# Softmax normalisation on the probabilities, and modulation in four column groups, in a one-core AdaLN transformer block

## The chip, the cores and the metric

The kernel runs on one core of a Trainium2 chip. The metric is the time on the device in microseconds (us), the median of several runs. The engines are TensorE (PE; its weight loads are listed as PEld), VectorE (DVE), ScalarE (ACT), GpSimd (POOL) and SyncE (SP, which issues most DMA transfers). Each engine works through its own queue in order, and semaphores order the queues among each other.

## What is computed

The reference is one adaptive-layernorm block over x of shape 4 x 1024 x 512, all in float32. Cut to what matters here:

```python
mod = (silu(c) @ wmod).reshape(4, 6, 1, 512)          # c is 4 x 512
sa, ca, ga, sb, cb, gb = mod[:, 0], ..., mod[:, 5]
ga, gb = the same with absolute value at least 0.25
h = layernorm(x) * (1 + ca) + sa
q = h @ q_w.T + q_b        # 16 heads of 32
k, v = h @ k_w.T + k_b, h @ v_w.T + v_b   # one head of 32, shared by all 16
attn = softmax(causal(q k / sqrt(32)))
x = x + ga * ((attn v) @ o_w.T + o_b)
h = layernorm(x) * (1 + cb) + sb
x = x + gb * ffn(h)        # 512 -> 2 x 2048 -> 512, with Hadamard transforms and silu
```

The Hadamard transforms of the feed-forward are applied to its weights once, at the start of the kernel ("preparation").

## The kernel before

The rows of x are worked in 8 blocks of 512 (two per sequence), and each block in 4 query tiles of 128 rows. Attention takes its query tiles in units (class `Unit`): of 8 heads in block 0 and in the second block of each sequence, of 16 heads in the first blocks of the other sequences, 52 units in all. `kmax` is the number of keys that a tile sees, 128 to 1024. The unit's scores, 128 queries by `kmax` keys for each head, lie in one of two halves of the tile `p`.

The life of a unit goes through these streams:

- `scores` (L397): four heads at a time, PE multiplies in four row groups of 32 rows of the array into four PSUM banks. A new unit's scores wait until the unit before has been attended.
- `minima` (L418): DVE masks, negates and copies the scores from PSUM to `p`, and keeps the row minimum in `nm`.
- `exps` (L438): ScalarE exponentiates in place, head by head, and accumulates each row's sum into `den`.
- `turns` (L455): DVE transposes `p` in 32 x 32 squares, two heads at a time.
- `attend` (L482): PE multiplies by v in 16 tiles of 32 x 32; ScalarE copies the result to `oT` (L492).
- `finish`, once per query tile: PE folds four partial sums with the matrix `fold` (L520, four column groups). In parallel DVE takes the reciprocal of `den` (L510), POOL broadcasts it to 32 columns a head (`wrd`, L511), PE transposes that (L527) and ScalarE copies it out of PSUM (`rd`, L529). DVE multiplies both into `aT` (L531), and PE applies the output projection (L260, from `ow` and `aT`). `add` multiplies by the gate and adds to x on POOL.

Helper `full_mm` (L260) holds the accumulating matmuls of several streams: the kv and q projections, the output projection, the modulation, and gate and up of the feed-forward (`ps<-h2T,wgu`). The feed-forward runs over 16 halves of 256 rows, each in 16 steps: gate and up on PE, tanh on ScalarE (L824), two products on DVE (L826, L829), down on PE (L852). At most two gate steps may have a PSUM bank open.

In preparation the modulation matrix `wmod` comes in six parts of 512 x 512, one after the other with the weights, into three buffers in the second half of `p`. Stream `mods` computes four of the parts transposed (features on partitions: 16 matmuls with a moving operand of 4 columns, into `modT`) and two as rows (4 matmuls of 512 columns, the gates `ga` and `gb`). `butterflies` (L716) and `transforms` (L739 to L752) prepare the feed-forward's weights in two buffers `tmp`, and write them to DRAM.

The order of all this is not written out by hand. Every stream is a generator of operations `Op(engine, cost, emit, reads, writes)`, and the planner `Flow` picks while the kernel is built: among the operations that could start within 0.3 us of the earliest, on that operation's engine, the one with the lowest rank. Ranks are given to the streams at the end (`multiply` 0, `finish` 3, `minima` and `scores` 4, `turns` 7, `exps` 8, gate and up 12). Costs are estimates such as `act_cost(n)` = 0.285 + 0.00083 n us. Thus one changed operation moves others on all queues.

Of the kernel before, what the change touches and what calls it, by code (L numbers as in the profile page):

```python
# [16 lines left out]
B, S, D = 4, 1024, 512  # L17
H, HD = 16, 32
FF = 2048
P = 128  # L20
# [140 lines left out]
def adaln_block(ctx, tc, x_d, small_d, const_d, wmod_d, qwT_d, kwT_d, vwT_d, vb_d, owT_d, ob_d,  # L161
# [10 lines left out]
    def sb(name, *shape):  # L172
        return outer.tile([P, *shape], F32, name=name)
# [15 lines left out]
    modT = sb("modT", 4, NDC, B)  # L189
    sc2, bi2 = sb("sc2", NDC, B), sb("bi2", NDC, B)  # L190
    cg, wgh, qbs = sb("cg", NFC), sb("wgh", NFC), sb("qbs", NDC)
    scT = sb("scT", NDC, B)
    kT = sb("kT", S)
    vT = sb("vT", TB)
    vrep = sb("vrep", S // 32, HD)
# [10 lines left out]
    nm = sb("nm", NNM, 2, 4)  # L206
    den = sb("den", 4, H)
    oT = sb("oT", 4, H, 32)
    rden, wrd, rd = sb("rden", H), sb("wrd", D), sb("rd", D)
    aT = sb("aT", 2, NDC, P)  # L210
    ga, y, y2 = sb("ga", D), sb("y", 2, D), sb("y2", D)

# [39 lines left out]
    def bk(b):  # L252
        return ("bank", b)
# [122 lines left out]
            for h0 in range(0, H, heads):  # L376
                units.append(Unit(len(units), i, ql, h0, heads))

    to_min, to_exp, to_turn, to_attend = deque(), deque(), deque(), deque()
    n_group = [0]  # L380

    def scores():
# [45 lines left out]
    def exps():  # L428
        while True:
            yield until(to_exp, "minima")  # L430
            if not to_exp:
                break
            u, c, slot = to_exp.popleft()
            ds = (u.i * NT + u.ql) % 4
            for j in range(4):
                h = c * 4 + j - u.h0
                e = u.head(h)
                yield Op("ACT", act_cost(u.kmax) + 0.19, lambda: nc.scalar.activation(  # L438
                    e, e, AF.Exp, bias=nm[:, slot, u.t, j:j + 1], scale=-1.0,
                    accum_out=den[:, ds, c * 4 + j:c * 4 + j + 1]),  # L440
                    [("nm", slot, j)], [u.key(h), ("den", ds)])
                if j % 2:
                    to_turn.append((u, h - 1))
        over["exps"] = True

    def turns():


        while True:
            yield until(to_turn, "exps")  # L450
# [51 lines left out]
    def finish():  # L502

        while True:
            yield until(to_finish, "attend")
            if not to_finish:
                break
            i, ql = to_finish.popleft()
            ds, a = (i * NT + ql) % 4, ql % 2
            yield Op("DVE", 0.2, lambda: nc.vector.reciprocal(rden, den[:, ds, :]), [("den", ds)], ["rden"])  # L510
            yield Op("POOL", 0.62, lambda: nc.gpsimd.tensor_copy(  # L511
                wrd.rearrange("p (h d) -> p h d", d=HD), rden.unsqueeze(2).to_broadcast([P, H, HD])),
                ["rden"], ["wrd"])
            yield banks.have(2)
            bo, br = banks.take(2)

            def folds():
                for c in range(NDC):
                    for j, r in enumerate(rows):
                        nc.tensor.matmul(ps[r, bo, c * P:(c + 1) * P], fold, oT[:, :, 4 * c + j, :],  # L520
                                         start=True, stop=True)
            yield Op("PE", 0.95, folds, ["oT"], [bk(bo)], mode="cols")
            st.folded += 1

            def turn():
                for c in range(NDC):
                    nc.tensor.transpose(ps[:, br, c * P:(c + 1) * P], wrd[:, c * P:(c + 1) * P], ident)  # L527
# [108 lines left out]
    def mods():  # L636
        for _ in range(6):
            yield lambda: bool(to_mod)
            part, s = to_mod.popleft()
            wm = raws[s]  # L640
            yield banks.have(1)
            o, = banks.take(1)
            if part in (2, 5):
                g = part // 5
                pg = ps[0:4, o, :]
                yield Op("PE", mm(512, 4), lambda: full_mm(pg, [(scT[:, k, :], wm[:, k, :]) for k in range(NDC)]),
                         [("raw", s)], [bk(o)], mode="full")
                busy[s] = False
                yield lambda: any(tmp_free)
                ts = tmp_free.index(True)  # L650
                tmp_free[ts] = False
# [12 lines left out]
                yield Op("DVE", 3.5, emit, [bk(o)], [("tmp", ts)])  # L664
                yield load(0.01, gates_d[g], gate, [("gates", g)], [("tmp", ts)])
                tmp_free[ts] = True
            else:
                slot = {0: 0, 1: 1, 3: 2, 4: 3}[part]
                pm = ps[:, o, 0:NDC * B].rearrange("p (a b) -> p a b", b=B)

                def products():
                    for dc in range(NDC):
                        full_mm(pm[:, dc, :], [(wm[:, k, dc * P:(dc + 1) * P], scT[:, k, :]) for k in range(NDC)])
                yield Op("PE", 3.5, products, [("raw", s)], [bk(o)], mode="full")
                busy[s] = False
                yield Op("DVE", 0.2, lambda: nc.vector.tensor_scalar_add(modT[:, slot], pm, 1.0 if slot in (1, 3) else 0.0),
                         [bk(o)], [f"mod{part}"])
            banks.give(o)
# [181 lines left out]
    def outputs():  # L860
# [81 lines left out]
```

## Time and profile before

| | |
|---|---|
| median of 3 runs | 2203.12 us (2201.21 to 2204.9) |
| profiled execution | 2202.49 us |
| its span, first to last instruction | 2200.7 us |
| mean granted TensorE clock | 0.997 |
| ACT exponentials (L438) | 512, 391.1 us busy |
| PE transposes of `wrd` (L527) | 128, 273 ns median |
| DMA | 257.09 MB, mean 117 GB/s |

A line of the profile's groups reads: line, engine, operation, output<-inputs, shapes and number; then busy us in all and mean ns of one; then the engine's idle time just before them, and what ended most of it. In the timeline the first number is the start in us, the second the us it covers. A float32 matmul stands in the profile as two records, so four matmuls are eight records; a transpose is one. Busy times of PE overlap, because matmuls are pipelined; the distance from one start to the next is what PE spends. PEclk is the share of its full clock that TensorE was granted.

### The profile page before, as it was taken

The numbers are of one execution on the slowest core, as the hardware profiler recorded it, in microseconds if no ns is written. First come the engines' busy times: TensorE is split into PE (matmuls) and PEld (weight loads), VectorE is DVE, ScalarE is ACT, GpSimd is POOL, SyncE is SP. The second block draws the span as 40 slices with busy tenths as digits, with TensorE's granted clock in tenths as the row PEclk, the third lists the DMA queues.
The fourth block names the chain that finished last, engine by engine and source line by source line (L and its number), as shares of the span: only waits on it lengthen the run. The fifth ranks groups of instructions, "written<-read, shape, count | busy, mean of one in ns | idle before, by whom it ended". The sixth has DMA issues, their size and how long they took to land.

```text
span 2200.7 us, 41314 instructions
## 1 busy us (share of the span) xinstructions
PE 2172.7 (99%) x17264; PEld 1374.5 (62%) x17264; DVE 1156.3 (53%) x2691; ACT 745.7 (34%) x1739; POOL 196.7 (9%) x197
## 2 busy tenths in 40 slices
PE   7999999999999999999999999999999999999998
PEld 4545666566556666556766656656766666777776
DVE  2476757645746686265246666364236767122111
ACT  2464434335534343253134333442123343111000
POOL 1032001000110010011001001011000101000000
PEclk9999999999999999999999999999999999999999
DMA  7542423223313342232523223223523332355453
GB/s 241 205 146 86 155 92 111 97 92 101 97 58 97 109 132 87 68 109 89 172 87 103 95 88 121 82 92 115 178 95 102 111 98 92 124 163 159 157 158 109
DMA packets 115602, 257.09 MB, mean 117 GB/s; under 512 B 11724, under 2 KB 28236, under 8 KB 115416
## 3 DMA queue, kind: packets, MB, share of 16 engines
q1 hardware_dynamic: 112392, 251.76, 35.8%
q8 instruction: 136, 2.23, 0.4%
q10 hardware_dynamic: 3024, 2.69, 0.4%
q14 instruction: 50, 0.41, 0.1%
HBM read 233.42 MB, written 20.99 MB: 116 GB/s over the span
## 4 chain that ended last, share of the span: by engine, by line
PE 98%; DVE 1%; issue 0%; DMA 0%; ACT 0%; SPq 0%; POOLq 0%; POOL 0%; DVEq 0%; ACTq 0%
PE ps L260 54%; PE ps L852 21%; PE ps L482 8%; PE ps L397 7%; PE ps L520 1%; PE ps L289 1%; PE ps L745 1%; PE ps L746 1%; PE ps L527 1%; PE ps L739 1%; PE ps L742 1%; DMA p<-in_wmod 0%; DVE tmp L716 0%; DVE p L418 0%; DVE p L455 0%
## 5 line engine op out<-in xcount | busy, mean ns | idle before, releaser
L260 PE MATMUL ps<-h2T,wgu 128*128 128x256 f32 x4096 | 949.2, 382 | 0.0
L260 PEld LDWEIGHTS ps<-h2T,wgu 128*128 128x128 f32 x4096 | 765.2, 190 | 236.0 <-issue 136.5
L852 PE MATMUL ps<-wd,g 128*128 128x512 f32 x1024 | 488.2, 601 | 0.7 <-DVE p L455 0.7
L438 ACT ACTIVATE p<-p,nm 128x512 f32<-128x512 f32 (+7 forms) x512 | 391.1, 766 | 175.2 <-DVE nm L418 175.2
L824 ACT ACTIVATE th<-ps,wgh 128x256 f32<-128x256 f32 x256 | 121.4, 474 | 804.6 <-PE ps L260 789.9
L826 DVE SCALAR_TENSOR_TENSOR th<-th,ps 128x256 f32<-128x256 f32 x256 | 106.6, 416 | 518.6 <-ACT th L824 518.6
L455 DVE STREAM_TRANSPOSE p<-p 128x256 f32<-128x256 f32 (+7 forms) x256 | 342.8, 1362 | 22.8 <-ACT p L438 21.7
L418 DVE CUSTOM_DVE_ANT_0 p<-ps,maskw 128x512 f32<-128x512 f32 (+3 forms) x512 | 273.6, 585 | 117.3 <-PE ps L397 116.1
L852 PEld LDWEIGHTS ps<-wd,g 128*128 128x128 f32 x1024 | 186.4, 190 | 185.5 <-issue 166.5
L482 PE MATMUL ps<-p,vrep 32*32 32x256 f32 (+1 forms) x8256 | 193.6, 409 | 5.9 <-issue 5.4
L397 PE MATMUL ps<-kT,qT 32*128 32x512 f32 (+3 forms) x1536 | 180.0, 533 | 2.3 <-DVE nm L418 1.0
L482 PEld LDWEIGHTS ps<-p,vrep 32*32 32x32 f32 x8256 | 119.8, 103 | 75.5 <-issue 32.2
L418 DVE CUSTOM_DVE_ANT_0 p<-ps,maskw,nm 128x128 f32<-128x128 f32 (+3 forms) x256 | 126.9, 546 | 67.6 <-PE ps L397 66.9
L492 ACT COPY oT<-ps 128x256 f32<-128x256 f32 (+1 forms) x208 | 74.7, 432 | 184.2 <-PE ps L482 183.5
L829 DVE SCALAR_TENSOR_TENSOR g<-th,cg,ps 128x256 f32<-128x256 f32 x256 | 123.1, 481 | 9.0
L397 PEld LDWEIGHTS ps<-kT,qT 32*128 32x128 f32 x1536 | 61.2, 183 | 103.9 <-issue 76.0
L260 PE MATMUL ps<-hT,qw 128*128 128x512 f32 x256 | 119.3, 610 | 0.0
L260 PE MATMUL ps<-ow,aT 128*128 128x512 f32 x256 | 115.8, 595 | 0.0
L511 POOL COPY wrd<-rden 128x512 f32<-128x512 f32 x32 | 19.6, 612 | 880.7 <-DVE rden L510 772.2
L438 ACT ACTIVATION_READ_ACCUMULATOR p<-p,nm 128x1 f32 x512 | 96.5, 188 | 0.0
L877 POOL TENSOR_TENSOR xs<-xs,y 128x512 f32<-128x512 f32 x32 | 40.6, 1269 | 507.6 <-DVE y L872 507.6
L260 PEld LDWEIGHTS ps<-hT,qw 128*128 128x128 f32 x256 | 49.6, 196 | 54.4 <-issue 53.7
(82 smaller groups left out, 1017.0 us busy)
## 6 DMA issues: line engine op xcount, KB each, us to landing
wgu<-wgu_d SPq DMA_DIRECT2D x256, 512.0 KB, 3.3
wd<-wd_d SPq DMA_DIRECT2D x256, 256.0 KB, 2.7
xs<-in_x SPq DMA_DIRECT2D x32, 256.0 KB, 4.7
out<-xs SPq DMA_DIRECT2D x32, 256.0 KB, 2.5
p<-in_wmod SPq DMA_DIRECT2D x6, 1024.0 KB, 8.3
p<-in_wgT SPq DMA_DIRECT2D x4, 1024.0 KB, 6.8
p<-in_wupT SPq DMA_DIRECT2D x4, 1024.0 KB, 5.0
wgu_d<-wo SPq DMA_DIRECT2D x4, 1024.0 KB, 4.2
```

Of the source, the lines that this page charges most:

```text
L260: nc.tensor.matmul(out, l, r, start=(k == 0), stop=(k == len(pairs) - 1))
L397: nc.tensor.matmul(ps[:, bb[j], 0:n], qT[r, c, u.ql * P:(u.ql + 1) * P], kT[r, kb * 512:kb * 512 + n], start=True, stop=True)
L418: yield Op("DVE", 0.245 + 0.00103 * n, lambda: nc.vector.tensor_tensor_reduce(o, ps[:, bb[j], 0:n], m, -1.0, nm[:, slot, 0, j:j + 1] if kb ...
L438: yield Op("ACT", act_cost(u.kmax) + 0.19, lambda: nc.scalar.activation(e, e, AF.Exp, bias=nm[:, slot, u.t, j:j + 1], scale=-1.0, accum_ou ...
L455: yield Op("DVE", 0.135 + 0.00105 * 2 * u.kmax, lambda: nc.vector.transpose(e, e), [], [u.key(h), u.key(h + 1)])
L482: nc.tensor.matmul(ps[rows[c], bb[g], 0:w], vrep[rows[g], 4 * kt + c, :], pv[rows[g], :, k:k + 32], start=(kt == 0), stop=(kt == nkt - 1))
L492: yield Op("ACT", act_cost(w), lambda: nc.scalar.copy(oT[:, g, u.h0:u.h0 + u.heads, :], ps[:, bb[g], 0:w].rearrange("p (h q) -> p h q", q= ...
L824: yield Op("ACT", act_cost(HB), lambda: nc.scalar.activation(th, pg, AF.Tanh, scale=wgh[:, f:f + 1]), [bk(o)], [("th", ts)])
L826: yield Op("DVE", 0.46, lambda: nc.vector.scalar_tensor_tensor(th, th, 1.0, pg, ALU.add, ALU.mult), [bk(o)], [("th", ts)])
L829: yield Op("DVE", 0.46, lambda: nc.vector.scalar_tensor_tensor(g, th, cg[:, f:f + 1], pu, ALU.mult, ALU.mult), [bk(o), ("th", ts)], [("g", ...
L852: nc.tensor.matmul(ps[:, acc[j], :], ff["g"][:, k % NG, j * P:(j + 1) * P], ff["wd"][:, k % NWD, :], start=(f == 0), stop=(f == NFC - 1))
L877: yield Op("POOL", 1.3, lambda: nc.gpsimd.tensor_add(x, x, y2), ["y2"], [xk])
```

## The change

The softmax is normalised earlier. After the four exponentials of a group of heads DVE takes the reciprocals of their four sums, and a new stream `scales` multiplies the exponentials in place on ScalarE, one activation with a per-partition scale for each head, ahead of the transpose. `finish` then has nothing to multiply: a ScalarE copy brings the folded result to `aT`. The reciprocals of 16, the POOL broadcast, the four PE transposes, their ScalarE copy and the DVE product go.

The modulation is computed the other way round. For all six parts four matmuls stand side by side in four column groups, each with a 128-row chunk of the silu (padded with zeros to 32 columns) as the stationary operand and 512 columns of `wmod` as the moving one. ScalarE copies the four partial results to a `tmp` buffer, and a matmul with `fold` adds them up: one of 512 columns for the gates, four of 4 columns for the parts that are needed transposed. Each part now holds one of the two `tmp` buffers from the copy to its end.

```diff
-    scT = sb("scT", NDC, B)
+    scT = sb("scT", NDC, HD)
...
-    rden, wrd, rd = sb("rden", H), sb("wrd", D), sb("rd", D)
+    rden = sb("rden", 4, H)
...
-    nc.scalar.activation(scT.rearrange("p a b -> p (a b)"), small[:, C_CT:C_CT + 16], AF.Silu)
+    nc.gpsimd.memset(scT, 0.0)
+    nc.scalar.activation(scT[:, :, 0:B], small[:, C_CT:C_CT + 16].rearrange("p (a b) -> p a b", b=B), AF.Silu)
...
+            yield Op("DVE", 0.2, lambda: nc.vector.reciprocal(rden[:, ds, cols], den[:, ds, cols]),
+                     [dk], [("rden", ds, c)])
+            to_scale.append((u, c, ds))
+        over["exps"] = True
+
+    def scales():
+
+        while True:
+            yield until(to_scale, "exps")
+            if not to_scale:
+                break
+            u, c, ds = to_scale.popleft()
+            for j in range(4):
+                h = c * 4 + j - u.h0
+                e = u.head(h)
+                yield Op("ACT", act_cost(u.kmax), lambda: nc.scalar.activation(
+                    e, e, AF.Copy, scale=rden[:, ds, c * 4 + j:c * 4 + j + 1]),
+                    [("rden", ds, c)], [u.key(h)])
                 if j % 2:
                     to_turn.append((u, h - 1))
-        over["exps"] = True
+        over["scales"] = True
...
-            yield Op("DVE", 0.2, lambda: nc.vector.reciprocal(rden, den[:, ds, :]), [("den", ds)], ["rden"])
-            yield Op("POOL", 0.62, lambda: nc.gpsimd.tensor_copy(
-                wrd.rearrange("p (h d) -> p h d", d=HD), rden.unsqueeze(2).to_broadcast([P, H, HD])),
-                ["rden"], ["wrd"])
-            yield banks.have(2)
-            bo, br = banks.take(2)
+            yield banks.have(1)
+            bo, = banks.take(1)
...
-            def turn():
-                for c in range(NDC):
-                    nc.tensor.transpose(ps[:, br, c * P:(c + 1) * P], wrd[:, c * P:(c + 1) * P], ident)
-            yield Op("PE", 0.48, turn, ["wrd"], [bk(br)], mode="full")
-            yield Op("ACT", 0.6, lambda: nc.scalar.copy(rd, ps[:, br, :]), [bk(br)], ["rd"])
-            banks.give(br)
-            yield Op("DVE", 0.7, lambda: nc.vector.tensor_mul(
-                aT[:, a], ps[:, bo, :].rearrange("p (c q) -> p c q", c=NDC),
-                rd.rearrange("p (c q) -> p c q", c=NDC)), [bk(bo), "rd"], [("aT", a)])
+            yield Op("ACT", act_cost(512), lambda: nc.scalar.copy(
+                aT[:, a], ps[:, bo, :].rearrange("p (c q) -> p c q", c=NDC)), [bk(bo)], [("aT", a)])
...
+            def products():
+                for k, r in enumerate(rows):
+                    nc.tensor.matmul(ps[r, o, :], scT[:, k, :], wm[:, k, :], start=True, stop=True)
+            yield Op("PE", mm(512), products, [("raw", s)], [bk(o)], mode="cols")
+            busy[s] = False
+            yield lambda: any(tmp_free)
+            ts = tmp_free.index(True)
+            tmp_free[ts] = False
+            m = tmp[:, ts, 0, :]
+            yield Op("ACT", act_cost(512), lambda: nc.scalar.copy(m, ps[:, o, :]), [bk(o)], [("tmp", ts)])
...
-                yield Op("PE", mm(512, 4), lambda: full_mm(pg, [(scT[:, k, :], wm[:, k, :]) for k in range(NDC)]),
-                         [("raw", s)], [bk(o)], mode="full")
+                yield Op("PE", mm(512), lambda: nc.tensor.matmul(pg, fold[:, 0:B], m, start=True, stop=True),
+                         [("tmp", ts)], [bk(o)], mode="full")
...
-                def products():
+                def turned():
                     for dc in range(NDC):
-                        full_mm(pm[:, dc, :], [(wm[:, k, dc * P:(dc + 1) * P], scT[:, k, :]) for k in range(NDC)])
-                yield Op("PE", 3.5, products, [("raw", s)], [bk(o)], mode="full")
-                busy[s] = False
+                        nc.tensor.matmul(pm[:, dc, :], m[:, dc * P:(dc + 1) * P], fold[:, 0:B], start=True, stop=True)
+                yield Op("PE", 0.9, turned, [("tmp", ts)], [bk(o)], mode="full")
...
-        (7, turns), (8, exps), (5, butterflies), (4.5, transforms), (10, load_wgu), (10, load_wd),
+        (7, turns), (8, exps), (7.5, scales), (5, butterflies), (4.5, transforms), (10, load_wgu), (10, load_wd),
```

More of the change, by code (lines that the diff above doesn't have):

```diff
@@ L377, in adaln_block @@
                 units.append(Unit(len(units), i, ql, h0, heads))
-    to_min, to_exp, to_turn, to_attend = deque(), deque(), deque(), deque()
+    to_min, to_exp, to_scale, to_turn, to_attend = deque(), deque(), deque(), deque(), deque()
     n_group = [0]
@@ L434, in exps @@
             ds = (u.i * NT + u.ql) % 4
+            dk = ("den", ds, c)
+            cols = slice(c * 4, c * 4 + 4)
             for j in range(4):
@@ L440, in exps @@
                     accum_out=den[:, ds, c * 4 + j:c * 4 + j + 1]),
-                    [("nm", slot, j)], [u.key(h), ("den", ds)])
+                    [("nm", slot, j)], [u.key(h), dk])
+            yield Op("DVE", 0.2, lambda: nc.vector.reciprocal(rden[:, ds, cols], den[:, ds, cols]),
[14 more added lines that the diff above has]
+                    [("rden", ds, c)], [u.key(h)])
                 if j % 2:
                     to_turn.append((u, h - 1))
-        over["exps"] = True
+        over["scales"] = True
     def turns():
         while True:
-            yield until(to_turn, "exps")
+            yield until(to_turn, "scales")
             if not to_turn:
@@ L508, in finish @@
             i, ql = to_finish.popleft()
-            ds, a = (i * NT + ql) % 4, ql % 2
-            yield Op("DVE", 0.2, lambda: nc.vector.reciprocal(rden, den[:, ds, :]), [("den", ds)], ["rden"])
-            yield Op("POOL", 0.62, lambda: nc.gpsimd.tensor_copy(
-                wrd.rearrange("p (h d) -> p h d", d=HD), rden.unsqueeze(2).to_broadcast([P, H, HD])),
-                ["rden"], ["wrd"])
-            yield banks.have(2)
-            bo, br = banks.take(2)
+            a = ql % 2
+            yield banks.have(1)
+            bo, = banks.take(1)
             def folds():
@@ L645, in mods @@
                 pg = ps[0:4, o, :]
-                yield Op("PE", mm(512, 4), lambda: full_mm(pg, [(scT[:, k, :], wm[:, k, :]) for k in range(NDC)]),
-                         [("raw", s)], [bk(o)], mode="full")
-                busy[s] = False
-                yield lambda: any(tmp_free)
-                ts = tmp_free.index(True)
-                tmp_free[ts] = False
+                yield Op("PE", mm(512), lambda: nc.tensor.matmul(pg, fold[:, 0:B], m, start=True, stop=True),
+                         [("tmp", ts)], [bk(o)], mode="full")
                 sgn, mag, gate = (tmp[0:4, ts, j, :] for j in range(3))
@@ L665, in mods @@
                 yield load(0.01, gates_d[g], gate, [("gates", g)], [("tmp", ts)])
-                tmp_free[ts] = True
             else:
@@ L669, in mods @@
                 pm = ps[:, o, 0:NDC * B].rearrange("p (a b) -> p a b", b=B)
-                def products():
+                def turned():
                     for dc in range(NDC):
-                        full_mm(pm[:, dc, :], [(wm[:, k, dc * P:(dc + 1) * P], scT[:, k, :]) for k in range(NDC)])
-                yield Op("PE", 3.5, products, [("raw", s)], [bk(o)], mode="full")
-                busy[s] = False
+                        nc.tensor.matmul(pm[:, dc, :], m[:, dc * P:(dc + 1) * P], fold[:, 0:B], start=True, stop=True)
+                yield Op("PE", 0.9, turned, [("tmp", ts)], [bk(o)], mode="full")
                 yield Op("DVE", 0.2, lambda: nc.vector.tensor_scalar_add(modT[:, slot], pm, 1.0 if slot in (1, 3) else 0.0),
                          [bk(o)], [f"mod{part}"])
+            tmp_free[ts] = True
             banks.give(o)
```

## The prediction

> **What bounds the kernel now.** I read the page's first part, then the chain that ended last, then the waits of PE.
>
> ```profile
> PE 2172.7 (99%) x17264; PEld 1374.5 (62%) x17264; DVE 1156.3 (53%) x2691; ACT 745.7 (34%) x1739; POOL 196.7 (9%) x197
> PE 98%; DVE 1%; issue 0%; DMA 0%; ACT 0%; SPq 0%; POOLq 0%; POOL 0%; DVEq 0%; ACTq 0%
> ```
>
> ```profile
> PE ps L260 <- DMA p<-in_wmod: 11.5, 1, 11.5
> PE ps L482 <- issue: 5.4, 10, 1.6
> ```
>
> PE is busy 2172.7 of 2200.7 us, the chain is 98% PE, and apart from the first load (11.5 us) and the last outputs PE waits a few us in all. So a us of PE work removed is a us won, as long as PE gets no new waits. ScalarE (ACT) has 1455 us free, VectorE (DVE) 1044.
>
> A busy PE may still run slowly. A table of stretches shows where:
>
> ```profile
> core 0: us, PE busy (x) PEld busy (x) DVE busy (x) ACT busy (x) POOL busy (x), PEclk, DMA share, GB/s
> 11.45:32.00 20.55, 19.83 (x83) 17.19 (x84) 2.55 (x6) 3.80 (x8) 4.00 (x2) 1.00 0.70 245
> 54.00:74.00 20.00, 20.00 (x83) 12.88 (x82) 2.74 (x12) 1.70 (x2) 0.00 (x0) 0.74 0.53 181
> 100.00:150.00 50.00, 49.91 (x379) 22.80 (x378) 33.28 (x84) 33.49 (x87) 10.29 (x7) 1.00 0.59 192
> 150.00:200.00 50.00, 48.46 (x398) 26.09 (x408) 46.89 (x75) 26.38 (x61) 20.10 (x12) 1.00 0.28 85
> ```
>
> From 54 to 74 us PE is busy throughout, yet its granted clock is 0.74. The timeline there:
>
> ```profile
> 55.10 3.63 PE L260 MATMUL ps<-scT,p 128*128 128x4 f32 x32
> 58.59 5.38 PE L260 MATMUL ps<-hT,qw 128*128 128x512 f32 x8
> 63.81 4.62 PE L260 MATMUL ps<-scT,p 128*128 128x4 f32 x32
> 68.28 6.04 PE L260 MATMUL ps<-hT,qw 128*128 128x512 f32 x8
> ```
>
> The two projections (qw) take 5.22 and 5.98 us from start to next start; from 41.37 to 44.80, with the clock at 1.00, eight such records take 3.43. The slow clock follows the modulation's 128x4 matmuls. Below I cost PE work from start to next start, since busy times overlap.
>
> **What leaves PE.**
>
> The transposed reciprocals. In the timeline:
>
> ```profile
> 550.25 1.08 PE L520 MATMUL ps<-oT,fold 128*32 128x128 f32 x32
> 551.26 0.66 PE L527 MATMUL ps<-ident,wrd 128*128 128x128 f32 x4
> 551.76 3.62 PE L260 MATMUL ps<-h2T,wgu 128*128 128x256 f32 x16
> ```
>
> The four L527 transposes hold PE 0.50 us, 32 times: **16.0 us**. The POOL broadcast (L511, 19.6 us) and a reciprocal of 16 go too. The ScalarE copy to rd (586 ns x32) is replaced by a ScalarE copy to aT of the same size, so the fold's way to the output projection loses the DVE product (688 ns) and gains nothing.
>
> Modulation. Its six parts hold PE 6.82, 6.83, 4.70, 3.49, 4.47 and 3.52 us = 29.8. In the changed kernel each has four matmuls in four column groups. No 512-column one of these is in the trace; the nearest is the row-tiled L397, 1.07 us for eight records (702.49 to 703.56). L520 above speaks for overlap in column groups: its 32 records take 1.01 us, where L527's pace of 0.125 each would make 4.0. Bounds: 0.86 (one full matmul of 512, two records) and 3.43 (no overlap); I take 1.07, and twice that while the clock is at half, as it is for the first three parts. Then four parts have four 128x4 matmuls, eight records at 109 ns (3.49 / 32) = 0.87 us, two have one fold of 512 columns = 0.86. Sum: 2 x (2.14 + 1.75) + (2.14 + 1.72) + 2 x (1.07 + 0.87) + (1.07 + 0.86) = 17.4. Saved **12.4 us**.
>
> Clock. The two slow projections lose 5.22 + 5.98 - 2 x 3.43 = 4.3 us. The Trainium skill (TensorE: Matmul & The Clock Gate, Part 1) says that the gate follows how busy PE was in a window of about 3.4 us. By that rule a PE that is 100% busy would not slow down and I would book nothing; the row has 20.00 of 20.00 busy at 0.74. I read it as 128x4 matmuls counting as little work; the changed kernel has a quarter as many. Ends 0 and 4.3; I take **2**.
>
> The changed kernel's own PE order has 535 changes of tile shape for 540. One costs about 0.1 us (eight gate records 1.82 us beside a change, 5.18 / 3 = 1.73 without): **0.5**.
>
> Together PE is relieved of 30.9 us.
>
> **What is added, and where it lies.**
>
> The scales: 512 ScalarE copies with a per-partition scale, 64 each of 128 to 1024 columns in steps of 128. Nearest row:
>
> ```profile
> L824 ACT ACTIVATE th<-ps,wgh 128x256 f32<-128x256 f32 x256 | 121.4, 474 | 804.6 <-PE ps L260 789.9 <-DVE nm L418 14.7
> L438 ACT ACTIVATE p<-p,nm 128x1024 f32<-128x1024 f32 x64 | 72.7, 1139 | 14.6 <-DVE nm L418 14.6
> L438 ACT ACTIVATE p<-p,nm 128x128 f32<-128x128 f32 x64 | 25.0, 393 | 13.8 <-DVE nm L418 13.8
> ```
>
> L824 also has one pointer operand: 474 ns at 256. The slope is (1139 - 393) / 896 = 0.833 ns a column. At the mean of 576 columns that is 0.741 us, so 379 us (from a plain copy's 383 ns at 256: 333; from L294's two pointers, 567: 427). ScalarE goes from 746 to about 1129 us, 51% of the span: not the bound over the whole.
>
> A rule speaks against this: the Trainium skill (ScalarE: Activation LUTs, Rules for kernel authors) puts multiplications on VectorE. By it the scales would follow L280, 562 to 604 ns for 512 f32 columns, some 0.65 us each and 330 us, on the engine that has 1156 already; the rows make that 50 us less work but 1486 on the fuller engine. ScalarE is the better place here, and I book the 379 there.
>
> The waits. A scale waits for a reciprocal of its four heads (128 of them on DVE, 0.22 us at most each by L510; with the products gone DVE's sum hardly moves), and the reciprocal waits for the fourth exponential. Behind a waiting scale on ScalarE stand the next exponentials, the copies that free PSUM banks and the tanh of the feed-forward, and PE waits for the last two. Behind the reciprocal on DVE stand minima, transposes and the gate products. The planner places all of it (scales at 7.5, between transposes and exponentials).
>
> From about 200 us on, PE has feed-forward work to put into attention's waits: 256 steps of 3.43 (gate and up) and 1.72 (down), 1318 us. I added durations along the changed order: from attention unit to unit PE has 18 to 128 us of work and ScalarE 9 to 46, each time less than PE. For a second block of a sequence the scales are 64 x 0.954 = 61 us; the 250 us from 650 to 900 hold 95 us of ScalarE now, so 156. Cover is there; without it all 379 us would show. I book **3 us** (0 to 20).
>
> Before 200 us there is no feed-forward to fill in. From 50 to 200 us ScalarE has 77 us and DVE 103. Block 0's scales add 16 x (0.37 + 0.47 + 0.58 + 0.69) = 34, so ScalarE gets to 111 of 150, and along the changed order the seven steps between the first and the eighth attention unit have 118 us of PE, 108 of ScalarE, 100 of DVE. Three nearly full engines in a chain don't mesh perfectly: **5 us** (0 to 17, half of the 34).
>
> Start. Each modulation part now goes PE, ScalarE copy, PE. The first copy lies under eight transposes; the second does not: 0.6 us and two hand-offs, 1.0. On ScalarE's queue the DMA issues of half of vb, of qw and of had, at 6.5 to 11.3 us now, come to stand behind both copies and the first hT activation, which waits for the second part, about 22.5 us. qw lands 10.2 us after its issue, so 32.7; the kv projection would end near 30.1. Together **3.5 us**. The extra memset of scT (0.2 us on POOL) ends before small lands.
>
> Sum: 30.9 - 3.5 - 5 - 3 = 19.4. The profiled execution took 2202.5 us (1.8 beside its span), so 2183.1; the median of the runs is 0.6 higher: **2184 us**.
>
> **Rivals.**
>
> *No new wait at all, and the clock stays up*: 16.0 + 12.4 + 4.3 + 0.5 = 33.2, so 2170. For: PE hardly waits anywhere now. Against: the start.
>
> *The stretch before the feed-forward becomes ScalarE's*: 17 us in place of 5: 2196. For: 108 against 118. Against: DVE at 46.89 of 50 cost PE only 1.5 us.
>
> *Column groups don't overlap*, so the change doesn't do what it says: 6 x (3.43 - 1.07) = 14 us back: 2198. L520 speaks against it.
>
> *Slower: the hand-off ScalarE to DVE to ScalarE stalls the tanh behind it.* There are 128. Exponentials that wait for the minima now wait 1.7 us on average (175.2 / 104). If a quarter of such a wait gets to PE each time, that is 54 us: 2184 - 3 + 54 = 2235. From (19.4 + 3) / 128 = 0.175 us a hand-off it eats the whole gain. Against: two gate banks may be open, and the second group is 3.43 us of PE work, twice the wait.
>
> **How the numbers follow.** Chances: forecast 0.57, no wait 0.12, ScalarE early 0.16, no overlap 0.04, slower 0.11. A measurement of this kernel tells about 0.2% (4.4 us) from no change. The third and fourth case lie near that edge: half of ScalarE-early and three quarters of no-overlap count as faster. Faster 0.57 + 0.12 + 0.08 + 0.03 = 0.80, same 0.09, slower 0.11. Range 2170 to 2204.
>
> **What would show it.** Right: PE busy falls by 20 to 35 us, no L527, PE clock 1.00 from 54 to 74, ScalarE near 1130 us with scales near 741 ns, PE idle up by under 12 us and mostly before 200 us. Wrong: PE waiting for ScalarE or for the reciprocals after 200 us, gate matmuls idle before the tanh, the column products at 3 us, or a scale well over 0.8 us.

## The result and the profile after

The changed kernel took 2183.02 us (median of 4 runs, 2182.1 to 2185.91) beside 2202.16 for the kernel before (4 runs, 2200.67 to 2204.9): a ratio of 0.9914, interval 0.9897 to 0.9931, or 19.1 us less. Its profiled run took 2182.1 us with a span of 2180.0, where before it was 2202.49 and 2200.7.

First the page of the changed kernel: engines, the chain that ended last, and two groups of ScalarE.

```profile
PE 2142.6 (98%) x17076; PEld 1346.5 (62%) x17076; DVE 1150.5 (53%) x2755; ACT 1083.6 (50%) x2257; POOL 178.5 (8%) x166
PE 97%; DVE 1%; issue 1%; ACT 1%; DMA 0%; SPq 0%; POOLq 0%; POOL 0%; DVEq 0%; ACTq 0%
L460 ACT ACTIVATE p<-p,rden 128x512 f32<-128x512 f32 (+7 forms) x512 | 359.2, 766 | 37.1 <-DVE rden L445 36.7
L840 ACT ACTIVATE th<-ps,wgh 128x256 f32<-128x256 f32 x256 | 121.4, 474 | 684.5 <-PE ps L261 673.9
```

PE is busy 30.1 us less and still carries the chain. The scales take 766 ns each. ScalarE has 338 us more busy time, and the tanh (L840, formerly L824) still waits for PE and not the other way round. No matmul waits for a scale. These are PE's longest waits (us in all, times, longest); the rest are 1.1 us or less each and name no scale either:

```profile
PE ps L656 <- DMA p<-in_wmod: 11.1, 1, 11.1
PE ps L503 <- issue: 10.0, 15, 1.5
PE ps L755 <- DVE tmp L732: 2.1, 1, 2.1
PE ps L290 <- DVE xha L281: 1.9, 1, 1.9
PE ps L755 <- POOL tmp L732: 1.6, 1, 1.6
```

The attends' "issue" (L503, formerly L482) has grown from 5.4 to 10.0 us, and the Hadamard matmuls of the preparation (L755) now wait for the butterflies (L732). By stretches, in the columns of the table of stretches before:

```profile
54.00:74.00 20.00, 19.53 (x96) 9.12 (x95) 11.80 (x50) 13.47 (x39) 2.41 (x4) 1.00 0.66 240
100.00:150.00 50.00, 48.20 (x299) 22.79 (x298) 43.30 (x86) 33.76 (x87) 19.66 (x11) 1.00 0.53 151
150.00:200.00 50.00, 46.10 (x488) 25.89 (x487) 36.20 (x60) 35.21 (x76) 10.65 (x5) 0.97 0.42 133
```

From 54 to 74 us the clock is 1.00 where it was 0.74. From 100 to 200 us PE idles 5.7 us where it idled 1.6, and the clock drops once. The timeline of PE shows the start (one line of the kernel before, then the changed kernel) and one such wait:

```profile
27.56 2.21 PE L289 MATMUL ps<-ident,xha 128*128 128x128 f32 x8 [0.72 <-DVE xha L280]
```

```profile
11.12 1.93 PE L656 MATMUL ps<-p,scT 128*32 128x512 f32 x8 [11.12 <-DMA p<-in_wmod]
19.08 1.87 PE L689 MATMUL ps<-fold,tmp 128*128 128x4 f32 x8 [0.76 <-ACT tmp L663]
22.87 2.21 PE L290 MATMUL ps<-ident,xha 128*128 128x128 f32 x8 [1.93 <-DVE xha L281]
55.81 1.06 PE L656 MATMUL ps<-p,scT 128*32 128x512 f32 x8
62.53 1.05 PE L689 MATMUL ps<-fold,tmp 128*128 128x4 f32 x8
170.28 1.87 PE L755 MATMUL ps<-tmp,had 128*128 128x512 f32 x2 [2.11 <-DVE tmp L732]
```

The column groups take 1.93 us at half clock and 1.06 at full: they do run side by side. At 170.28 PE has just waited 2.11 us, and two records that need 0.86 at full clock take 1.87.

**An account of PE's time.** To compare kernels I sum, over each whole trace, PE's work at fixed paces read from undisturbed rows (109 ns for a record of up to 128 columns, 0.838 ns a column above, 1.07 us for eight row-tiled records of 512 columns and less for fewer, 1.0 for eight in column groups, 20.6 ns for an attend record of 256, 0.094 us a change of tile shape). The excess is what the starts show beyond it: waits, lost clock, and whatever these paces price too low. Only its differences between kernels count. I split it at 100 and 210 us. "Half clock" is what the stretches after 210 us at a clock of 0.5 lose, half their length. "Attend gaps" are distances over 0.4 us between two neighbouring records of one attend. All in us; the rows from e1 on are the experiments below.

| kernel | work | excess to 100 | 100 to 210 | after 210 | of it attend gaps | of it half clock | the rest after 210 |
|---|---|---|---|---|---|---|---|
| before | 2111.0 | 19.0 | 5.3 | 43.8 | 10.8 | 0 | 33.0 |
| changed | 2086.3 | 12.1 | 11.8 | 48.6 | 16.7 | 0 | 31.9 |
| changed, run again | 2086.3 | 13.0 | 11.9 | 50.2 | 18.1 | 0 | 32.1 |
| e1 softmax only | 2095.0 | 18.3 | 11.8 | 49.0 | 13.6 | 3.4 | 32.0 |
| e2 modulation only | 2101.9 | 12.2 | 7.8 | 49.8 | 15.2 | 1.7 | 32.9 |
| e3 no scales, same order | 2086.3 | 11.6 | 9.0 | 52.8 | 17.8 | 3.4 | 31.6 |
| e4 padded | 2111.0 | 8.6 | 5.2 | 44.7 | 11.3 | 0 | 33.4 |
| e5 unplanned | 2085.9 | 13.3 | 5.6 | 61.4 | 18.7 | 8.5 | 34.2 |
| e6 second scale, late | 2085.7 | 10.3 | 11.9 | 45.4 | 14.1 | 0 | 31.3 |
| e7 second scale, first | 2086.1 | 13.6 | 18.5 | 53.2 | 16.0 | 5.1 | 32.1 |
| e10 dearer | 2085.8 | 11.6 | 10.2 | 53.6 | 13.5 | 6.8 | 33.3 |

From before to changed that is -24.7 of work, -6.9 ahead of 100 us, +6.5 from 100 to 210, +4.8 after it, and -0.3 because the first matmul starts earlier: -20.6 of the -20.7 us of span. The last column hardly moves (31.3 to 34.2) whatever ScalarE has to do. It is not time lost: from 210 to 2190 us PE idles only 6.3 us in the kernel before, most of it at the attends, so the column must be work that the fixed paces price too low. After 210 us these kernels differ by attend gaps and clock, and by at most 3 us of anything else.

**What the attend gaps are.** PE's timeline at one of them in the changed kernel, weight loads and matmuls:

```profile
1868.31 3.45 PEld L503 LDWEIGHTS ps<-p,vrep 32*32 32x32 f32 x182 [0.33 <-issue]
1868.31 3.93 PE L503 MATMUL ps<-p,vrep 32*32 32x256 f32 x182
1873.74 1.46 PEld L503 LDWEIGHTS ps<-p,vrep 32*32 32x32 f32 x74 [1.98 <-issue]
1873.74 1.94 PE L503 MATMUL ps<-p,vrep 32*32 32x256 f32 x74 [1.50 <-issue]
```

The 256 records of an attend are split: after 182 of them PE neither loads nor multiplies for more than a microsecond, and "issue" says that nothing in the trace released it. The view of DMA queues for the 10 us from 1866 shows what else happened (queue: packets, MB, share of the engines):

```profile
q8 instruction: 2, 0.03, 1.2%
```

An instruction fetch. One of the two packets lasted from 1871.6 to 1872.6 us, and PE went on 1.2 us after its end. There are 134 such packets in the run, one every 16 us. All 17 gaps of the changed kernel and all 14 of the kernel before end 1.2 to 1.6 us after such a packet, and so do all 204 gaps in the fourteen traces of this case (0.4 to 2.8 us long, 1.06 in the mean); a band of 0.4 us in 16 would catch 3 in 100 by accident. Attends have one matmul record per 20 ns, the densest stream here, and in the changed kernel "issue" holds PE in no other line.

The records' places settle it. Each packet has 16384 bytes, and there is one per about 257 records of PE's queue (34508 records of matmuls, weight loads and PE's sequencer for 134 packets; 34897 for 136 before): the fetches bring PE's instructions, in blocks of 256. Counted along this queue from its start, every one of the 204 gaps ends at record 193 or 194 of a block of 256. I read it as PE having used up a block and waiting for the next. The gaps follow blocks that PE passed quickly: in the changed kernel 24 blocks that end inside an attend took it under 3 us, and 17 of them end in a gap; of the 45 that took longer none does. Run e9 below moves the blocks: it keeps the changed kernel's order of matmuls and puts 96 records in front. None of its 16 gaps falls on a matmul where the changed kernel has one, 8 fall exactly 48 matmuls earlier (96 records), and all 16 again at record 193 or 194.

The gaps also carry the late clock drops. Of the 13 stretches of half clock after 210 us in the fourteen traces, 12 begin between 0.4 us before and 2.0 us after the end of an attend gap of 1.69 us or more; the other is that of e5 at 215.7 us. Not every such gap brings a drop: 12 of 26 do.

### The profile page after: what moved, and what is told of

Same layout as the page of the kernel before. It is cut to its first block, busy times and chain, and to the rows that moved or that the text cites. A ratio compares the mean times of both kernels' runs of the same rounds, so it can differ in the third digit from the quotient of the medians.

```text
span 2180.0 us, 41200 instructions
## 1 busy us (share of the span) xinstructions
PE 2142.6 (98%) x17076; PEld 1346.5 (62%) x17076; DVE 1150.5 (53%) x2755; ACT 1083.6 (50%) x2257; POOL 178.5 (8%) x166
## 4 chain that ended last, share of the span: by engine, by line
PE 97%; DVE 1%; issue 1%; ACT 1%; DMA 0%; SPq 0%; POOLq 0%; POOL 0%; DVEq 0%; ACTq 0%
PE ps L261 53%; PE ps L868 21%; PE ps L503 9%; PE ps L398 7%; PE ps L537 1%; PE ps L290 1%; PE ps L761 1%; PE ps L762 1%; PE ps L656 0%; PE ps L755 0%; DMA p<-in_wmod 0%; PE ps L758 0%; DVE tmp L732 0%; DVE p L419 0%; PE ps L689 0%
## 5 line engine op out<-in xcount | busy, mean ns | idle before, releaser
L840 ACT ACTIVATE th<-ps,wgh 128x256 f32<-128x256 f32 x256 | 121.4, 474 | 684.5 <-PE ps L261 673.9
L460 ACT ACTIVATE p<-p,rden 128x512 f32<-128x512 f32 (+7 forms) x512 | 359.2, 766 | 37.1 <-DVE rden L445 36.7
L503 PE MATMUL ps<-p,vrep 32*32 32x256 f32 (+1 forms) x8256 | 194.4, 409 | 10.3 <-issue 10.0
L503 PEld LDWEIGHTS ps<-p,vrep 32*32 32x32 f32 x8256 | 119.6, 103 | 83.3 <-issue 32.7
L566 POOL TENSOR_TENSOR y<-y,ga 128x512 f32<-128x512 f32 x32 | 40.7, 1273 | 1043.2 <-DVE y L550 952.8
L398 PEld LDWEIGHTS ps<-kT,qT 32*128 32x128 f32 x1536 | 61.4, 183 | 92.1 <-issue 69.4
```

Source lines behind the costliest of these rows:

```text
L398: nc.tensor.matmul(ps[:, bb[j], 0:n], qT[r, c, u.ql * P:(u.ql + 1) * P], kT[r, kb * 512:kb * 512 + n], start=True, stop=True)
L460: yield Op("ACT", act_cost(u.kmax), lambda: nc.scalar.activation(e, e, AF.Copy, scale=rden[:, ds, c * 4 + j:c * 4 + j + 1]), [("rden", ds, ...
L503: nc.tensor.matmul(ps[rows[c], bb[g], 0:w], vrep[rows[g], 4 * kt + c, :], pv[rows[g], :, k:k + 32], start=(kt == 0), stop=(kt == nkt - 1))
L840: yield Op("ACT", act_cost(HB), lambda: nc.scalar.activation(th, pg, AF.Tanh, scale=wgh[:, f:f + 1]), [bk(o)], [("th", ts)])
```

## The experiments

Each was compared with the kernel before on the same chip; the medians of before were 2205.43 us (e1 to e4), 2204.18 (e5 to e7 and the changed kernel again) and 2206.11 (e8 to e11).

**e1, the softmax part alone.** To the kernel before come all softmax hunks of the change, with this at their core, and none of the modulation's:

```diff
+                yield Op("ACT", act_cost(u.kmax), lambda: nc.scalar.activation(
+                    e, e, AF.Copy, scale=rden[:, ds, c * 4 + j:c * 4 + j + 1]),
```

> Only the softmax part of the change; the modulation is that of the kernel before. Theory (both parts pay, PE work removed less new waits): the transposes' 16.0 us go, waits of some 8 us come, so 8 us below before, about 2194. Rival 1 (the scales eat their own gain, the modulation brought everything): 2202, no change. Rival 2 (the softmax part brought everything): 2183.

Measured 2192.81 us (2190.32 to 2196.99), 0.9944, interval 0.9931 to 0.9956: 12.6 us less, which excludes both rivals. PE's work is down by 16.0, the transposes and their changes of shape; 6.5 us of excess from 100 to 210 us and 5.2 after it have come, in a profiled run that was the longest of its five.

**e2, the modulation alone.** All modulation hunks, with these at their core, and none of the softmax:

```diff
-                yield Op("PE", 3.5, products, [("raw", s)], [bk(o)], mode="full")
+            yield Op("PE", mm(512), products, [("raw", s)], [bk(o)], mode="cols")
+                yield Op("PE", 0.9, turned, [("tmp", ts)], [bk(o)], mode="full")
```

> Only the modulation part; the softmax is that of the kernel before. Theory with the sizes of the trace after: PE 14 us less for the parts, 4.3 us for the two projections that no longer run at half clock, less 2.7 us of waits at the start: 15.7 us below before, about 2186.5. By the terms of the prediction (12.4 + 2 - 3.5) 11 us, about 2191. Rival 1: 2183. Rival 2: 2202. If the parts add up, the two gains together give the 19 us of the whole change.

Measured 2197.84 us (2195.2 to 2198.91), 0.9964, interval 0.9951 to 0.9976: 7.6 us less. The two parts add up to 20.2; the whole change gave 19.1, and 20.8 when run again. The modulation alone gave less than its terms (11 us, or 15.7 with the sizes of the trace after). The table says where the rest went: -9.1 of work and -6.8 ahead of 100 us, but +2.5 from 100 to 210 and +6.0 after it, 4.4 of that in attend gaps. Its operations are all early; the late part comes with the order, which the planner wrote anew, and with where the blocks of instructions fall in it.

**e3, the changed order without the scales.** The operations stay in the plan and issue nothing:

```diff
-            yield Op("DVE", 0.2, lambda: nc.vector.reciprocal(rden[:, ds, cols], den[:, ds, cols]),
+            yield Op("DVE", 0.2, lambda: None,
-                yield Op("ACT", act_cost(u.kmax), lambda: nc.scalar.activation(
-                    e, e, AF.Copy, scale=rden[:, ds, c * 4 + j:c * 4 + j + 1]),
+                yield Op("ACT", act_cost(u.kmax), lambda: None,
```

> The changed kernel in the same planned order on every queue, but the 512 scales and the 128 reciprocals are not issued, so the probabilities stay unnormalised: that part of the computation is left out. ScalarE falls to about 710 us. Theory: the scales lie under PE almost everywhere, and what they cost is waits of 5 to 10 us, mostly before 200 us: 2173 to 2178. Rival (they are fully hidden, and the waits come from the planned order): 2183. Rival (the hand-offs leak all along): below 2165.

Measured 2181.89 us (2180.98 to 2182.92), 0.9893, interval 0.9879 to 0.9906, which overlaps that of the changed kernel. The waits of PE in e3 (its lines stand one lower):

```profile
PE ps L502 <- issue: 11.3, 16, 1.4
PE ps L754 <- DVE tmp L731: 2.1, 1, 2.1
PE ps L754 <- POOL tmp L731: 1.6, 1, 1.6
```

ScalarE is at 742.3 us, and both waits for butterflies are still there, to the tenth of a microsecond; the attends' issue has not shrunk either. So my theory of 5 to 10 us fell and the rival (fully hidden, 2183) held: the scales cost next to nothing by being executed, and the waits belong to the order that the plan made around them.

**e4, the kernel before with its moving operand padded.** The 4 columns are broadcast to 128; beside the lines shown only the PSUM tile and the DVE instruction that reads its first 4 columns are laid out to match:

```diff
-                        full_mm(pm[:, dc, :], [(wm[:, k, dc * P:(dc + 1) * P], scT[:, k, :]) for k in range(NDC)])
+                        full_mm(pm[:, dc], [(wm[:, k, dc * P:(dc + 1) * P],
+                                             scT[:, k, :].unsqueeze(1).to_broadcast([P, P // B, B]))
+                                            for k in range(NDC)])
```

> The kernel before, with the moving operand of the four transposed modulation parts repeated 32 times, 128 columns in place of 4, of which only the first 4 are used. PE's pace in these matmuls should stay near 109 ns a record[...]. Theory (matmuls of 4 columns count as little work for the clock): the granted clock is 1.00 from 54 to 74 us, the part at 64 us and the two projections win 5.3 us, the first two parts perhaps some of their 6.8 us each: 2195 to 2198. Rival (the clock falls for another reason, such as weight loads at this pace): same dips, 2202.

Measured 2197.0 us (2192.57 to 2199.71), 0.9961, interval 0.9949 to 0.9974. The stretch that was at 0.74, and two parts in the timeline of e4:

```profile
54.00:74.00 20.00, 19.54 (x90) 9.82 (x89) 7.14 (x35) 6.86 (x20) 0.00 (x0) 1.00 0.66 231
```

```profile
17.85 3.74 PE L260 MATMUL ps<-scT,p 128*128 128x128 f32 x32
49.21 3.73 PE L260 MATMUL ps<-scT,p 128*128 128x128 f32 x32
52.78 3.60 PE L260 MATMUL ps<-hT,qw 128*128 128x512 f32 x8
```

32 times the arithmetic at the same pace: the part at 49.21 holds PE 3.57 us, where the one of 4 columns at 55.10 held it 3.49. The projection behind it is at full clock, and the clock is full from 15.7 us on, where before it was from 32.1, with drops at 59.4 and 66.2. Padding brings as much as the whole new modulation (e2), without its 9.1 us less of work.

**e5, the scales out of the plan as well.** As e3, but the two operations are not yielded at all:

```diff
-            yield Op("DVE", 0.2, lambda: nc.vector.reciprocal(rden[:, ds, cols], den[:, ds, cols]),
-                     [dk], [("rden", ds, c)])
-                yield Op("ACT", act_cost(u.kmax), lambda: nc.scalar.activation(
-                    e, e, AF.Copy, scale=rden[:, ds, c * 4 + j:c * 4 + j + 1]),
-                    [("rden", ds, c)], [u.key(h)])
```

> The changed kernel without the scales and their reciprocals, and without them in the plan as well (the probabilities stay unnormalised: that part of the computation is left out). The planner now orders everything as if they did not exist. Theory after e3 (the scales cost nothing where they stand, the new waits of PE come from the order that was planned around them): PE waits fall back towards those of before, 5 to 8 us below the changed kernel, about 0.988 of before. Rival (the waits come from the modulation's order or from chance of the plan): as the changed kernel, 0.991.

Measured 2188.83 us (2186.64 to 2189.52), 0.993, interval 0.9917 to 0.9942. The changed kernel in the same comparison, as a control:

> The changed kernel again, as it is, beside the runs of this call, so that they are compared with it on one chip. Both theories: 0.991 of before.

It took 2183.34 us (2182.45 to 2184.14), 0.9906, interval 0.9891 to 0.9921. So my theory that the order around the scales costs 5 to 8 us fell: without them it is 5.5 us slower, each of its five runs above each of the control's four. The table shows both halves of this. From 100 to 210 us the excess is 5.6, that of before; with the scales in the plan it is 9.0 without executing them (e3) and 11.8 with. After 210 us the new order loses 8.5 us to half clock, in one stretch of 10.2 us at 215.7 and two of 3.4, and 18.7 in attend gaps.

**e6 and e7, twice the scales.** A second activation by 1.0 behind each scale, in e6 for all blocks but the first, in e7 (`u.i == 0`) in the first alone:

```diff
+    ones = sb("ones", 1)
+    nc.gpsimd.memset(ones, 1.0)
+                if u.i > 0:
+                    yield Op("ACT", act_cost(u.kmax), lambda: nc.scalar.activation(
+                        e, e, AF.Copy, scale=ones[:, 0:1]), [], [u.key(h)])
```

> The changed kernel with every scale of blocks 1 to 7 followed by a second one by 1.0 on ScalarE: 448 more, some 345 us more of ScalarE, which then has about 1430 us. Theory (after 200 us feed-forward work covers ScalarE): 0 to 5 us above the changed kernel. Rival (the hand-off and the tanh behind it leak to PE): 345 us more should then cost 20 us or more.

> The changed kernel with a second scale by 1.0 in block 0 only: 64 more, 34 us more of ScalarE, in the stretch before the feed-forward. Theory (no cover there, three engines nearly full: ScalarE would have 142 us against 118 of PE between the first and the eighth attention unit): 12 to 24 us above the changed kernel. Rival (the stretch has slack, or the planner fills it with feed-forward sooner): 0 to 4 us.

e6 took 2175.36 us (2174.92 to 2176.31), 0.9872, interval 0.9858 to 0.9885. Its page:

```profile
PE 2137.6 (98%) x17076; PEld 1345.0 (62%) x17076; DVE 1158.0 (53%) x2755; ACT 1428.1 (66%) x2705; POOL 178.5 (8%) x167
```

345 us more of ScalarE, and 8 us faster than the changed kernel. By the table, 4.0 of the 8.2 us between their profiled spans are fewer attend gaps, 2.7 lie ahead of 100 us, 0.6 are changes of tile shape, 0.8 the rest. The recorded expectation had nothing below the changed kernel's time. The order is another one, because the plan's costs are, but only from 246 us on; up to there PE's order is that of the changed kernel. So the 2.7 us are not the order: the clock came to full at 24.9 us in this profiled run and at 28.8 in the control's.

e7 took 2190.18 us (2186.76 to 2194.07), 0.9942, interval 0.9929 to 0.9955: 34 us of ScalarE in the first block cost 6.8, more than the rival allowed and little over half of the least that the theory had. There PE does wait once for long, by the profile until a scale (L462 of e7), before the first gate matmul at 183.9 us:

```profile
PE ps L263 <- ACT p L462: 5.3, 1, 5.3
```

So ahead of the feed-forward about a fifth of ScalarE's added work reaches the time; behind it, ten times as much did not. In both runs the order changed as well, so neither figure is ScalarE's alone.

**e8, the scales on VectorE**, as the rule that the prediction weighed would have it:

```diff
-                yield Op("ACT", act_cost(u.kmax), lambda: nc.scalar.activation(
-                    e, e, AF.Copy, scale=rden[:, ds, c * 4 + j:c * 4 + j + 1]),
+                yield Op("DVE", 0.07 + 0.00105 * u.kmax, lambda: nc.vector.tensor_scalar_mul(
+                    e, e, rden[:, ds, c * 4 + j:c * 4 + j + 1]),
```

> The changed kernel with the 512 scales on VectorE in place of ScalarE (a tensor_scalar by the same reciprocals, planned at 0.07 + 0.00105 us a column). ScalarE falls to about 710 us, VectorE rises from 1150 to some 1480. Theory (what counts is the stretch before the feed-forward, where VectorE has 100 of 118 us already; 34 us more on ScalarE there cost 7 us in e7): 26 us more on the fuller engine cost 4 to 12 us there, 2186 to 2196, and nothing later. The rule that multiplications belong on VectorE: no slower than the changed kernel, 2176 to 2184.

Measured 2188.93 us (2185.81 to 2190.39), 0.9919, interval 0.9903 to 0.9934, which overlaps that of the changed kernel. The time lies in the theory's range, but the kernel before was slower on this chip too; by the ratio either engine will do. VectorE needs 308 ns at 128 columns and 760 at 1024, ScalarE 392 and 1141; my 0.65 us at 576 columns was too high.

**e9, PE kept busy until the first load lands.** 24 multiplications of the identity by itself at the start, into a bank not in use:

```diff
+    for _ in range(24):
+        nc.tensor.matmul(ps[:, 7, 0:P], ident, ident, start=True, stop=True)
```

> The changed kernel with 24 idle matmuls of 128 columns (identity by identity into a PSUM bank that nobody reads) while PE waits for the first part of wmod, about 2 to 11 us. Theory (the clock follows PE's work; at the start it is at half until 27 us): full clock before 11 us, the first three parts and the transposes win about 5 us, 2176 to 2180. Rival (those us are hidden behind DMA and the chain of copies and norms at the start): 2182 to 2184.

Measured 2183.21 us (2180.54 to 2186.14), 0.9899, interval 0.9882 to 0.9916. PE in the timeline of e9:

```profile
11.34 1.06 PE L658 MATMUL ps<-p,scT 128*32 128x512 f32 x8 [1.68 <-DMA p<-in_wmod]
21.32 2.21 PE L292 MATMUL ps<-ident,xha 128*128 128x128 f32 x8 [4.00 <-DVE xha L283]
```

The first part now runs at full clock (1.06 for 1.93), and what that wins, PE waits for the normalised input (4.00 for 1.93 us); the clock falls back meanwhile. The kv projection starts 1.5 us earlier. So the rival held: at the start PE is not the only engine of the chain.

**e10 and e11, only the plan's costs.** To see whether e6's gain was its order, the scales of all blocks but the first are planned at twice their cost and issued once; e11 is that with e9's start:

```diff
-                yield Op("ACT", act_cost(u.kmax), lambda: nc.scalar.activation(
+                yield Op("ACT", act_cost(u.kmax) * (2 if u.i else 1), lambda: nc.scalar.activation(
```

> The changed kernel with the planned cost of a scale doubled for blocks 1 to 7, and each scale issued once as before: only the order changes. Theory after e3 and e6 (PE's waits follow the planned order, not ScalarE's load): as e6 or a little better, 0.986 to 0.988 of before, 2172 to 2177. Rival (e6 was faster for another reason, such as the start): as the changed kernel, 0.991.

> e9 and e10 together: the idle matmuls at the start and the doubled planned cost. If both hold and add up: 0.984 to 0.986 of before, 2167 to 2172, faster than both kernels. If only one holds: 0.986 to 0.989.

e10 took 2178.73 us (2177.28 to 2184.24), 0.9879, interval 0.986 to 0.9898; e11 2179.4 (2178.95 to 2179.83), 0.9877, interval 0.9862 to 0.9892. A false cost in the plan, with the same instructions, gives most of e6's 8 us. The two do not add up. The profiled run of e10 is its longest, with 6.8 us lost to half clock in four stretches after 210 us, each behind an attend gap; the drops alone are as large as its spread. e6, e10 and e11 are the fastest versions here, some 3 thousandths below the changed kernel. The interval of e6 lies below both that were measured for the changed kernel; that of e10 touches both and that of e11 the second, so for these two the gain is likely, not settled.

## Why the prediction was right, point by point

The forecast was 2184, the time is 2183.02, and it was right for the right reason in its large terms. Several small ones had the right size and the wrong cause, and a total within 1 us is luck: single terms were off by up to 2.3 us, and the order alone moved these kernels by 5 us.

| term | booked | in the trace |
|---|---|---|
| transposed reciprocals off PE | -16.0 | -16.0, none left |
| modulation | -12.4 | 29.8 became 15.7: -14.1 |
| clock of the projections | -2 (0 to -4.3) | -4.3 |
| changes of tile shape | -0.5 | 5 fewer (538 for 543), -0.5 at the same price |
| start | +3.5 | +2.0 |
| 100 to 200 us (booked: before 200) | +5 (0 to 17) | +5.8 |
| after 200 us | +3 (0 to 20) | +4.1 |
| sum | -19.4 | -23.0; span -20.7 |

The measured terms overshoot the span by 2.3 us, because they were read one by one; the account above closes to 0.1. In the row from 100 to 200 us, 4.1 are idle time of PE and 1.7 are lost in one clock drop.

*Transposes*: as booked, and e1 has 16.0 us less of work; that e1 gives 12.6 is the order's doing, not theirs.

*Modulation*: column groups overlap, 1.00 us for eight records at full clock and 1.86 at half, so the fourth case is out. The products of three parts ran at half clock, as booked; in sum it is 1.7 us better, since the row-tiled row that I took (1.07) was a little too dear, twice that at half clock too, and the third part's fold ran at full clock (0.95 us for 1.72).

*Clock*: the reading that narrow matmuls keep the clock low, against the rule of the Trainium skill (TensorE: Matmul & The Clock Gate, Part 1) by which a PE that is busy keeps its clock, was right: e4 shows it by the columns alone, with PE 20.00 of 20.00 us busy before and 19.54 when padded, and the clock at 0.74 and 1.00. I booked half of its upper end, and only for two projections. The clock at the start belongs to it too: e4 gets 10.4 us ahead of 100 us. (Ahead of its first record, at 32.1 us before and 27.2 in the changed kernel, the column PEclk reads 1.00; that the clock is at half there shows in the pace, 6.82 us for the 32 records that take 3.49 later.) The modulation's 7.6 us in e2 are no more than e4 gets without saving any work; e2's 9.1 us of work went into the gaps and waits counted above. The order does not fix the clock: e3 and e10, with the changed kernel's order of matmuls in this stretch, were at full clock earlier, from 23.7 and 24.6 us on, and dropped for 3.4 us at 61 and 62 us.

*Start*: PE waited 0.76 for the second copy and 1.2 more for the input. The wait for qw did not come; kv and qw ran from 26.88 to 33.97 us without a gap. That sub-term, 2.6 us, was wrong.

*Before 200 us*: the size was right by luck, the step was wrong. I booked three nearly full engines that mesh badly because of block 0's scales. e3 has the order without the scales and the same waits. They are waits for the butterflies on VectorE and GpSimd, where the plan that reserves time for the scales has put them (e5, unplanned, has none of them), and, in the changed kernel, one drop of the clock right behind such a wait. That ScalarE is near its edge there fits e7.

*After 200 us*: cover was there, far more than I granted. The last column of the table moves by 3 us while ScalarE's load goes from 742 to 1428, and e3, without the 128 hand-offs, is hardly faster; so the slower rival, a leak at each hand-off, is refuted. The 4.1 us more of idle lie in attend gaps, 16.7 us for 10.8: waits for instructions, of which the prediction had no term. That they came to about the booked 3 us is luck.

*PE idle* rose by 9.4 us (28.0 to 37.4), within the 12 that I gave, but only about half of it ahead of 200 us, where I had looked for most.

*ScalarE*: 1083.6 us for 1129, though each scale took 766 ns and not 741: back-to-back activations overlap in the busy sum (512 x 0.766 = 392, in the group 359.2).

What stays open: the order decides which blocks of instructions fall inside attends, but why 7 of the 24 quick blocks of the changed kernel end without a gap, and 14 of the 26 long gaps bring no drop of the clock, is not shown. Of most kernels one trace was read. The softmax part together with the padded modulation of e4 was not run, so which of the two modulations is the better one beside it is not known.

## What to carry to other kernels

Where one engine is 98% busy, count what leaves it from start to next start, and expect most of that sum: here 24.7 us of work less gave 19.1 to 20.8. Work that went to an engine with half its time free cost nothing measurable where the first had other work to put in, and about a fifth of itself where it had not. Look at narrow matmuls for the clock they cost behind them: more columns at the same pace can be faster than less work. When a planner rewrites the order, allow 5 to 8 us either way for a kernel like this, see where the blocks of instructions fall in its densest streams, and run the order without the operation before putting a wait down to the operation.

## What the runs showed of the hardware that was not expected

- A dense stream of small matmuls (one record per 20 ns) stops, for 1.06 us in the mean, where it runs out of a block of 256 instructions: all 204 gaps stand at record 193 or 194 of a block, and they cost 10.8 to 18.7 us a run. With 96 more records in front (e9) the gaps moved to other matmuls.
- Beside matmuls of 4 float32 columns the clock was at half (from 11.5 to 32.1 us, and in stretches from 59.4 and 66.2 us) although PE was busy (20.00 of 20.00 us from 54 to 74); with 128 columns they took the same time, and the clock was full from 15.7 us on.
- The clock drops in stretches of 3.4 us or a multiple (6.8, 10.2), each costing about half its length. In the changed kernel the one drop between 27.2 us and the last output stands at 170.5, right behind a wait of 2.11 us; after 210 us, 12 of 13 drops stand at a long attend gap.
- 345 us more work on ScalarE, to 66% of the span, did not lengthen the kernel.
